# The inverse transform's residual rows: from two row groups of 512 columns to four row groups of 256, with the heads' banks taken in turn

## The chip, the cores and the metric

The program runs on one core of a Trainium2 chip. The metric is the time on the device, in microseconds, of one execution of the whole program. Several runs of each kernel are taken, and their median is compared. One execution is also recorded by the hardware profiler, and the profile lines come from that one. Engines are named as in the profile: PE (TensorE's matmuls), PEld (its weight loads), DVE (VectorE), ACT (ScalarE), POOL (GpSimd), SP (the engine that issues most transfers). Times within an execution are counted from the start of its span.

## What is computed

The input is 128 graphs of 128 nodes with 256 channels each, and an adjacency matrix per graph. Two layers follow one another; each is added to its input. All arithmetic is float32.

```python
# layer 0
h = max(layernorm(x), 0)
x = x + L0(h, adj)
#   L0: xc = h^T;  c1 = relu(bn1(conv1d(xc, conv1_w, width 1)))
#       c2 = bn2(conv1d(c1, conv2_w, width 17, pad 8))
#       x_conv = relu(c2 + xc)^T
#       s = h @ w_se^T + b_se;  A = exp(-|s_n - s_m|^2) * adj
#       x_nmp = A @ relu(h @ w_msg^T + b_msg)
#       a GRU cell with input [x_conv, x_nmp] and state h gives the output
# layer 1: five graph convolutions on subsets of the first 25 nodes, weighted and summed
h = max(layernorm(x), 0)
x = x + L1(h, adj)
```

## The kernel before

The 128 graphs are worked in 32 blocks of four (`BB = 4`, `N = 128` nodes, `T = 512` columns, `H = 256`).

**The heads** (up to about 277 us). Block by block, `head_stats`, `head_norm`, `head_turn` and `head_conv1` do the layer norm, the transpose and the width-1 convolution; `head_spectra` takes the result to the frequency domain by a matmul with `fd`. In between, `some_spectra` runs one round of `weight_spectra` at a time: the taps of the width-17 convolution go to the frequency domain (L164, 17 rows, four row groups of the array into four banks; the copies out of the banks are L170 on DVE and L172 on ACT) and to DRAM as `vd`. `constants()` prepares the two batch norms: it has two steps, and the second one scales the weights `wc1` (L136) that `head_conv1` (L227) multiplies by. All of this stands under a manual schedule, so each engine works in the order written.

**The products per frequency** (277 to 455 us). `spectral` loads `v` from `vd`, multiplies for each of 68 frequency pairs, and writes `yd` (the first 128 of 136 rows) and `yrd` (the last eight, the residual rows).

**The main part** (from 455 us). For each block the GRU's gates are computed by seven products per unit (L636). Between two products the generator `beside_gates` does a step of the next block: `messages` (L522, emptied by L532 to L541), then `conv_out` in two steps, `edge_terms` (L560), `edges` (L572: four matmuls of 5 rows on four row groups, into four banks), `x_nmp` (L587); or a step of `back` (L800, L813) or of `layer1` (L904, L964).

`conv_out` is the inverse transform of the width-17 convolution: for each half `o` of the channels it sums the residual rows `yr` (eight per graph, times `idr`, L499) and the 128 main rows `ym` (times `idm`, L502) in one bank of PSUM, then DVE scales the bank and adds `ht` (L504), and ACT applies the relu (L505). In the kernel before, the residual rows of the four graphs lie in 32 partitions for each `o`; one matmul of 512 columns with a block-diagonal `idr` serves the four graphs. `load_y` loads `ym` and `yr` two blocks ahead.

PSUM has eight banks; `bank()` gives one. All of them come from one pool with eight buffers under one name. In the compiled program of the kernel before, a bank is given out again in the order in which banks come free in the compiler's plan, and PE's instructions stand in the order of the program text.

Of the kernel before, what the change touches and what calls it, by code (L numbers as in the profile page):

```python
# [8 lines left out]
F32 = mybir.dt.float32  # L9
# [4 lines left out]
P = 128  # L14
# [3 lines left out]
BB = 4  # L18
# [56 lines left out]
def gnn_kernel(ctx: ExitStack, tc: tile.TileContext, io, out0: bass.AP, out1: bass.AP):  # L75
# [8 lines left out]
    front = ExitStack()  # L84
    hc = front.enter_context(tc.tile_pool(name="hc", bufs=1))
    dram = ctx.enter_context(tc.tile_pool(name="dram", bufs=1, space=bass.MemoryType.DRAM))
    psum = ctx.enter_context(tc.tile_pool(name="psum", bufs=8, space=bass.MemoryType.PSUM))

    def bank():
        return psum.tile([P, 512], F32, tag="bank", name="bank")  # L90

    def row(name, n):

# [21 lines left out]
    def constants():  # L115


        for j, v0 in enumerate((V_BN1, V_BN2)):
            g, b, m, v = (vec[:, v0 + 2 * q:v0 + 2 * q + 2] for q in range(4))
            sc, sh = bn[:, j, 0, :], bn[:, j, 1, :]  # L120
            ve = cst.tile([P, C], F32, name=f"bnve{j}")
            nc.vector.tensor_scalar(ve, v, EPS, None, op0=ALU.add)
            rs = cst.tile([P, C], F32, name=f"bnrs{j}")
            nc.gpsimd.tensor_tensor(rs, ve, mhalf[:, :C], op=ALU.pow)
            nc.vector.tensor_mul(sc, g, rs)
            nc.vector.tensor_mul(ve, m, sc)
            nc.vector.tensor_sub(sh, b, ve)

        bnb = hc.tile([P, 2 * C, P], F32, name="bnb")
        nc.vector.tensor_copy(bnb, bn[:, 0].rearrange("p q c -> p (q c)")[:, :, None].to_broadcast([P, 2 * C, P]))  # L130
        yield
        psb = bank()
        for q in range(2 * C):
            nc.tensor.matmul(psb[:, q * P:(q + 1) * P], bnb[:, q, :], ident, start=True, stop=True)
        nc.scalar.copy(bnr.rearrange("p q d -> p (q d)"), psb)
        nc.vector.tensor_mul(wc1, wc1, bnr[:, 0:1, :].to_broadcast([P, C, D]))  # L136
        nc.vector.tensor_add(brz, vec[:, V_IH:V_IH + 4], vec[:, V_HH:V_HH + 4])
        yield

# [9 lines left out]
    def taps_load(pool, c, q, queue, split=1, amid=None):  # L149
        w2 = pool.tile([P, WCH // 4, P], F32, tag="w2", name="w2", bufs=3)  # L150
        for t in range(0, WCH // 4, WCH // 4 // split):
            queue.dma_start(w2[:, t:t + WCH // 4 // split], io["w2t"][:, c, q, t:t + WCH // 4 // split])
            if amid:
                amid.pop()()
        return w2
# [198 lines left out]
    with front as es:  # L354
# [9 lines left out]
        with ExitStack() as ws:  # L364

            ws.enter_context(tc.manual_schedule())

            xk = ws.enter_context(tc.tile_pool(name="xk", bufs=1, side="right"))
            wp = ws.enter_context(tc.tile_pool(name="wp", bufs=1))
            ahead = 4  # L370
            todo = [(c, q) for c in range(C) for q in range(D // WCH)]
            nc.scalar.dma_start(gt, io["gt"])
            nc.scalar.dma_start(vec, io["vec"])

            taps = [taps_load(wp, *todo[0], nc.sync, split=4, amid=[lambda: head_load(xk, ahead, 0, nc.sync)])]
            spectra = []

            def some_spectra(k=1):
                for _ in range(k):
                    if not spectra and todo:  # L380
                        spectra.append(weight_spectra(wp, *todo.pop(0), taps.pop(0)))
                    if spectra and next(spectra[0], STOP) is STOP:
                        spectra.pop(0)
                        if len(todo) > 2:
                            taps.append(taps_load(wp, *todo[2], nc.sync))
                        some_spectra()

            constant_loads()
            head_load(xk, ahead, 1, nc.sync)
            taps.append(taps_load(wp, *todo[1], nc.sync))  # L390
            for k in range(2, ahead):
                head_load(xk, ahead, k, nc.sync)
            nc.sync.dma_start(fw, row("fw", 5))
            taps.append(taps_load(wp, *todo[2], nc.sync))
            head_stats(hk, 0)
            some_spectra()
            head_norm(0)
            consts = constants()
            next(consts)
            some_spectra()  # L400
            some_spectra()
            head_turn(hk, 0)
            head_stats(hk, 1)
            some_spectra()
            next(consts)
            head_norm(1)
            head_stats(hk, 2)
            some_spectra()
            heads(hk, xk, ahead, X, some_spectra)
            while spectra or todo:  # L410
                some_spectra()

        bp = es.enter_context(tc.tile_pool(name="bp", bufs=1, reuse_waits="tile"))
        spectral(bp, (X0, 0), 0, NB, {})
# [46 lines left out]
    def load_y(i):  # L461
        g0 = i * BB
        yr = wk.tile([P, P], F32, tag="yr", name="yr", bufs=2)
        ym = wk.tile([P, BB, D], F32, tag="ym", name="ym", bufs=2)
        nc.sync.dma_start(ym, yd[g0:g0 + BB].rearrange("g r o -> r g o"))
        for o in range(C):
            nc.sync.dma_start(yr[o * BB * NR:(o + 1) * BB * NR, :],
                              yrd[g0:g0 + BB, :, o * P:(o + 1) * P].rearrange("g r o -> (g r) o"))
        loaded[i] = ym, yr

    fmx = cst.tile([P, 1], F32)
# [19 lines left out]
    def conv_out(i):  # L491

        ht = hts[i]
        ym, yr = loaded.pop(i)
        xc = wk.tile([P, C, T], F32, tag="xc", name="xc", bufs=2)
        pss = [bank() for _ in range(C)]
        for o, ps in enumerate(pss):
            g = slice(o * BB * NR, (o + 1) * BB * NR)
            nc.tensor.matmul(ps, yr[g, :], idr[g, :], start=True, stop=False)  # L499
        for o, ps in enumerate(pss):  # L500
            for b in range(BB):
                nc.tensor.matmul(ps[:, b * N:(b + 1) * N], ym[:, b, o * P:(o + 1) * P], idm,  # L502
                                 start=False, stop=b == BB - 1)
            nc.vector.scalar_tensor_tensor(xc[:, o, :], ps, sc2[:, o:o + 1], ht[:, o, :], op0=ALU.mult, op1=ALU.add)  # L504
            nc.scalar.activation(xc[:, o, :], xc[:, o, :], AF.Relu, bias=sh2[:, o:o + 1])  # L505
            yield
        xcs[i] = xc
# [505 lines left out]
    with tc.manual_schedule(engines={nc.gpsimd.engine}):  # L1013
# [2 lines left out]
        nc.gpsimd.memset(lr, 0.0)  # L1016
        nc.gpsimd.memset(lr[:, 0, :, 3:4], -1.0)
        nc.gpsimd.memset(lr[:, 1, :, 4:5], 1.0)
    idr = wk.tile([P, T], F32)
    nc.sync.dma_start(idr[:C * BB * NR], io["idr"])  # L1020

    load_y(0)
    load_y(1)
# [75 lines left out]
def _spectral_constants():  # L1099
# [24 lines left out]
    inv[0, 0], inv[0, 1] = c[0] / LW, c[NP_] / LW  # L1124
    inv[1:, 0], inv[1:, 1] = 2 * c[f] / LW, -2 * s[f] / LW
    inv = inv.reshape(LW, P)
    idr = np.zeros((2, BB, NR, BB, P))
    for b in range(BB):
        idr[:, b, :, b] = inv[P:]
    d = {"gt": gt.reshape(P, LW), "fd": fd.reshape(P, LW), "idm": inv[:P], "idr": idr.reshape(2 * BB * NR, BB * P)}  # L1130
    return {k: np.ascontiguousarray(v, dtype=np.float32) for k, v in d.items()}


# [86 lines left out]
```

## Time and profile before

| | |
|---|---|
| median of 3 runs | 1884.16 us (1883.59 to 1886.41) |
| the profiled execution | 1882.45 us |
| its span, first to last instruction | 1880.5 us |
| PE busy | 1858.3 us, 99% of the span |
| DVE, ACT, POOL busy | 1353.7, 743.4, 665.3 us |
| mean granted clock of TensorE | 0.998 |

A group's line in the profile reads: line of the code, engine, operation, output<-inputs, shapes, count, then busy time in us and mean ns of one, then the engine's idle time just before these instructions and what ended most of it. A float32 matmul leaves two records. "Released by" is inferred from semaphores. In the timeline each row has its start, its length, the engine and the line; in brackets stands the idle time before it and what ended it.

### The profile page before, as it was taken

How to read it: one execution, taken by the hardware profiler on the slowest of the kernel's cores; microseconds unless marked ns; L12 is line 12 of the kernel's file. 1: busy time of each engine (PE TensorE's matmuls, PEld its weight loads, DVE VectorE, ACT ScalarE, POOL GpSimd, SP SyncE). 2: the span in 40 equal slices, each digit the busy share in tenths (PEclk: the TensorE clock that was granted, in tenths of full speed). 3: DMA queues.
4: the chain of work that ended last, by engine and by line, in shares of the span. 5: the costliest groups of instructions: out<-in, count | busy, mean ns of one | idle time of the engine just before them, and what ended most of it. 6: DMA issues, size and time to landing. Idle time of an engine off the chain costs nothing.

```text
span 1880.5 us, 31012 instructions
## 1 busy us (share of the span) xinstructions
PE 1858.3 (99%) x10854; PEld 1593.0 (85%) x10854; DVE 1353.7 (72%) x3248; ACT 743.4 (40%) x1667; POOL 665.3 (35%) x803
## 2 busy tenths in 40 slices
PE   8999999999999999999999999999999999999998
PEld 6888888888888888888788888888788888888887
DVE  7787765455878888888656778787666678788643
ACT  4665651111443334333334433433343343334334
POOL 1111125676343544454212345444312344544200
PEclk9999999999999999999999999999999999999999
DMA  8878788997532233224234322333233333222125
GB/s 295 292 309 309 283 291 280 349 314 248 165 90 73 72 83 94 76 72 121 64 103 113 122 74 72 90 79 112 61 102 94 121 94 86 72 72 67 41 88 157
DMA packets 218330, 267.95 MB, mean 142 GB/s; under 512 B 105186, under 2 KB 181815, under 8 KB 216127
## 3 DMA queue, kind: packets, MB, share of 16 engines
q1 hardware_dynamic: 206079, 195.60, 36.1%
q10 hardware_dynamic: 12096, 70.36, 9.1%
q8 instruction: 87, 1.43, 0.3%
q14 instruction: 68, 0.56, 0.1%
HBM read 169.24 MB, written 96.67 MB: 141 GB/s over the span
## 4 chain that ended last, share of the span: by engine, by line
PE 93%; DVE 2%; DMA 2%; POOL 1%; issue 0%; SPq 0%; ACT 0%; DVEq 0%; POOLq 0%; ACTq 0%
PE bank L636 44%; PE bank L318 6%; PE bank L227 5%; PE bank L964 5%; PE bank L904 5%; PE bank L522 5%; PE bank L502 3%; PE bank L243 3%; PE bank L313 3%; PE bank L587 3%; PE bank L164 2%; PE bank L499 2%; PE bank L213 1%; PE bank L883 1%; PE bank L813 1%; PE bank L572 1%
## 5 line engine op out<-in xcount | busy, mean ns | idle before, releaser
L636 PE MATMUL bank<-t,sw 128*128 128x256 f32 x1152 | 290.9, 379 | 0.0
L649 POOL TENSOR_TENSOR u<-u,m 128x256 f32<-128x256 f32 x128 | 93.4, 730 | 499.2 <-ACT m L647 424.6
L636 PEld LDWEIGHTS bank<-t,sw 128*128 128x128 f32 x1152 | 210.6, 190 | 26.6 <-issue 2.3
L636 PE MATMUL bank<-t,wih 128*128 128x256 f32 x768 | 197.2, 379 | 0.0
L636 PEld LDWEIGHTS bank<-t,wih 128*128 128x128 f32 x768 | 143.4, 190 | 19.3 <-issue 0.5
L227 PE MATMUL bank<-wc,ht 128*128 128x256 f32 x512 | 125.5, 390 | 0.3 <-DVE wc L136 0.3
L310 POOL TENSOR_TENSOR vs<-v 128x256 f32<-128x256 f32 x134 | 98.1, 756 | 72.4 <-PE bank L313 38.1
L545 ACT ACTIVATE msg<-msg 128x512 f32<-128x512 f32 x64 | 36.9, 622 | 205.5 <-DVE msg L541 205.5
L636 PE MATMUL bank<-xc,wih 128*128 128x256 f32 x384 | 114.5, 380 | 0.0
L636 PE MATMUL bank<-t,whh 128*128 128x256 f32 x384 | 114.5, 380 | 0.0
L636 PE MATMUL bank<-xn,wih 128*128 128x256 f32 x384 | 114.2, 379 | 0.0
L964 PE MATMUL bank<-w,hh 128*125 128x256 f32 (+9 forms) x480 | 113.3, 379 | 0.0
L197 POOL TENSOR_TENSOR rs<-ve,mhalf 128x4 f32<-128x4 f32 x32 | 32.6, 1020 | 223.0 <-DVE ve L195 223.0
L636 PE MATMUL bank<-ht,whh 128*128 128x256 f32 x384 | 109.9, 380 | 0.0
L904 PE MATMUL bank<-ax,w 128*128 128x500 f32 (+8 forms) x416 | 107.0, 396 | 0.9 <-DMA w<-in_w_dram 0.9
L227 PEld LDWEIGHTS bank<-wc,ht 128*128 128x128 f32 x512 | 93.6, 192 | 15.3 <-DVE wc L136 0.6
L964 PEld LDWEIGHTS bank<-w,hh 128*125 128x125 f32 (+9 forms) x480 | 84.3, 177 | 18.0 <-issue 0.9
L682 ACT ACTIVATE nn<-nn,vec 128x512 f32<-128x512 f32 x64 | 46.2, 722 | 134.1 <-DVE nn L681 134.1
L307 DVE SCALAR_TENSOR_TENSOR s<-X 128x256 f32<-128x256 f32 x67 | 46.2, 691 | 66.5 <-PE bank L318 66.5
L654 DVE TENSOR_TENSOR u<-bank,u 128x256 f32<-128x256 f32 x128 | 53.5, 418 | 54.5 <-PE bank L636 54.2
L172 ACT COPY sp<-bank 128x272 f32<-128x272 f32 x208 | 66.7, 401 | 63.0 <-PE bank L164 61.9
L502 PEld LDWEIGHTS bank<-idm,ym 128*128 128x128 f32 x512 | 66.0, 196 | 26.4 <-issue 24.0
(206 smaller groups left out, 4449.0 us busy)
## 6 DMA issues: line engine op xcount, KB each, us to landing
vd<-sp ACTq DMA_DIRECT2D x16, 2176.0 KB
v<-vd SPq DMA_DIRECT2D x34, 1024.0 KB
w<-in_w_dram SPq DMA_DIRECT2D x40, 512.0 KB
ln<-in_x_dram SPq DMA_DIRECT2D x32, 512.0 KB
htd<-ht ACTq DMA_DIRECT2D x32, 512.0 KB
yd<-ys ACTq DMA_DIRECT2D x32, 512.0 KB
ht<-htd SPq DMA_DIRECT2D x32, 512.0 KB
ym<-yd SPq DMA_DIRECT2D x32, 512.0 KB
```

Of the source, the lines that this page charges most:

```text
L172: nc.scalar.copy(dst, s)
L227: nc.tensor.matmul(pv[:, bb, :], ht[:, c, b * N:(b + 1) * N], wc1[:, c, :], start=c == 0, stop=c == C - 1)
L243: nc.tensor.matmul(ps[:, bb * LW:(bb + 1) * LW], h1[:, 2 * h + bb, c * P:(c + 1) * P], fd, start=True, stop=True)
L310: nc.gpsimd.tensor_tensor(vs[:, c], vr[c], vi[c], op=ALU.add)
L313: nc.tensor.matmul(p1[:, :D], a[:, c], vs[:, c], start=c == 0, stop=c == C - 1)
L318: nc.tensor.matmul(ps[:, k * D:(k + 1) * D], u[:, c], w[c], start=c == 0, stop=c == C - 1)
L502: nc.tensor.matmul(ps[:, b * N:(b + 1) * N], ym[:, b, o * P:(o + 1) * P], idm, start=False, stop=b == BB - 1)
L522: nc.tensor.matmul(ps[:, b, :], d[:, b * N:(b + 1) * N], w, start=True, stop=True)
L636: nc.tensor.matmul(ps, w, d, start=n == 0, stop=n == len(pairs) - 1)
L649: nc.gpsimd.tensor_tensor(got["u4"], got["u2"], got["m5"], op=ALU.add)
L904: nc.tensor.matmul(pv[:, q - q0, :], w1s[k5 + g][:, c, q * P:(q + 1) * P], xv[:, c], start=c == 0, stop=c == C - 1)
L964: nc.tensor.matmul(ps[:n1, :D], hh[:, q, at:at + n1], w2s[k5 + g][:, q, :], start=q == 0, stop=q == HID // P - 1)
```

## The change

It has three parts.

1. `conv_out`: the residual rows of each half `o` are split again by pairs of graphs, `h`. The four groups of 16 rows start at partitions 0, 32, 64 and 96. Each is one matmul of 256 columns into a bank of its own, of which half is used. The main rows' matmuls go to the same four half banks, and DVE empties each half bank by itself. `load_y` loads `yr` in four pieces; `idr` is laid out for this.
2. In the heads, `bank()` takes eight single-buffer banks in turn; after the heads that pool is closed and one with eight buffers under one name, and waits for each buffer, is opened.
3. `constants()` has three steps now: the first batch norm's scales are computed ahead of the first `head_stats`, the scaled weights ahead of the first `head_norm`, and the second batch norm's scales after the third `head_stats`. One round of `some_spectra` ahead of `heads` is left out (the rounds after it make up for it).

```diff
-    psum = ctx.enter_context(tc.tile_pool(name="psum", bufs=8, space=bass.MemoryType.PSUM))
+    turns = ExitStack()
+    banks = [turns.enter_context(tc.tile_pool(name="turns", bufs=1, space=bass.MemoryType.PSUM)), 0]
     def bank():
-        return psum.tile([P, 512], F32, tag="bank", name="bank")
+        pool, n = banks
+        if n is None:
+            return pool.tile([P, 512], F32, tag="bank", name="bank")
+        banks[1] = (n + 1) % 8
+        return pool.tile([P, 512], F32, tag=f"bank{n}", name="bank")
...
     def constants():
-        for j, v0 in enumerate((V_BN1, V_BN2)):
+        def scales(j, v0):
...
+        scales(0, V_BN1)
         bnb = hc.tile([P, 2 * C, P], F32, name="bnb")
...
         nc.vector.tensor_mul(wc1, wc1, bnr[:, 0:1, :].to_broadcast([P, C, D]))
+        yield
+        scales(1, V_BN2)
         nc.vector.tensor_add(brz, vec[:, V_IH:V_IH + 4], vec[:, V_HH:V_HH + 4])
         yield
...
+            consts = constants()
+            next(consts)
             head_stats(hk, 0)
             some_spectra()
+            next(consts)
             head_norm(0)
-            consts = constants()
-            next(consts)
             some_spectra()
             some_spectra()
             head_turn(hk, 0)
             head_stats(hk, 1)
             some_spectra()
-            next(consts)
             head_norm(1)
             head_stats(hk, 2)
-            some_spectra()
+            next(consts)
             heads(hk, xk, ahead, X, some_spectra)
             while spectra or todo:
                 some_spectra()
+        turns.close()
+        banks[:] = [ctx.enter_context(tc.tile_pool(name="psum", bufs=8, space=bass.MemoryType.PSUM, reuse_waits="tile")), None]
...
         for o in range(C):
-            nc.sync.dma_start(yr[o * BB * NR:(o + 1) * BB * NR, :],
-                              yrd[g0:g0 + BB, :, o * P:(o + 1) * P].rearrange("g r o -> (g r) o"))
+            for h in range(2):
+                r0, g1 = 32 * (2 * o + h), g0 + 2 * h
+                nc.sync.dma_start(yr[r0:r0 + 2 * NR, :],
+                                  yrd[g1:g1 + 2, :, o * P:(o + 1) * P].rearrange("g r o -> (g r) o"))
...
-        pss = [bank() for _ in range(C)]
-        for o, ps in enumerate(pss):
-            g = slice(o * BB * NR, (o + 1) * BB * NR)
-            nc.tensor.matmul(ps, yr[g, :], idr[g, :], start=True, stop=False)
-        for o, ps in enumerate(pss):
-            for b in range(BB):
-                nc.tensor.matmul(ps[:, b * N:(b + 1) * N], ym[:, b, o * P:(o + 1) * P], idm,
-                                 start=False, stop=b == BB - 1)
-            nc.vector.scalar_tensor_tensor(xc[:, o, :], ps, sc2[:, o:o + 1], ht[:, o, :], op0=ALU.mult, op1=ALU.add)
+        pss = [[bank()[:, :H] for _ in range(2)] for _ in range(C)]
+        for o in range(C):
+            for h, ps in enumerate(pss[o]):
+                r0 = 32 * (2 * o + h)
+                g = slice(r0, r0 + 2 * NR)
+                nc.tensor.matmul(ps, yr[g, :], idr[g, :], start=True, stop=False)
+        for o in range(C):
+            for h, ps in enumerate(pss[o]):
+                for b in range(2):
+                    nc.tensor.matmul(ps[:, b * N:(b + 1) * N], ym[:, 2 * h + b, o * P:(o + 1) * P], idm,
+                                     start=False, stop=b == 1)
+                v = slice(h * H, (h + 1) * H)
+                nc.vector.scalar_tensor_tensor(xc[:, o, v], ps, sc2[:, o:o + 1], ht[:, o, v], op0=ALU.mult, op1=ALU.add)
             nc.scalar.activation(xc[:, o, :], xc[:, o, :], AF.Relu, bias=sh2[:, o:o + 1])
             yield
...
-    idr = wk.tile([P, T], F32)
-    nc.sync.dma_start(idr[:C * BB * NR], io["idr"])
+    idr = wk.tile([P, H], F32)
+    nc.sync.dma_start(idr, io["idr"])
...
-    idr = np.zeros((2, BB, NR, BB, P))
-    for b in range(BB):
-        idr[:, b, :, b] = inv[P:]
+    idr = np.zeros((4, 32, 2, P))
+    for b in range(2):
+        idr[:, b * NR:(b + 1) * NR, b] = inv[P:]
```

More of the change, by code (lines that the diff above doesn't have):

```diff
@@ L1126, in _spectral_constants @@
     inv = inv.reshape(LW, P)
[L1127 to L1130 removed]
+    idr = np.zeros((4, 32, 2, P))
+    for b in range(2):
+        idr[:, b * NR:(b + 1) * NR, b] = inv[P:]
+    d = {"gt": gt.reshape(P, LW), "fd": fd.reshape(P, LW), "idm": inv[:P], "idr": idr.reshape(P, 2 * P)}
     return {k: np.ascontiguousarray(v, dtype=np.float32) for k, v in d.items()}
```

## The prediction

> **What bounds the kernel now.** I read the page first: the busy shares and the chain that ended last.
>
> ```profile
> span 1880.5 us, 31012 instructions
> ...
> PE 1858.3 (99%) x10854; PEld 1593.0 (85%) x10854; DVE 1353.7 (72%) x3248; ACT 743.4 (40%) x1667; POOL 665.3 (35%) x803
> ...
> PE 93%; DVE 2%; DMA 2%; POOL 1%; issue 0%; SPq 0%; ACT 0%; DVEq 0%; POOLq 0%; ACTq 0%
> ```
>
> TensorE is the bound nearly everywhere, so a change pays by what it takes off PE's own sequence, and costs by what makes PE wait. Next come the groups kept apart by shape, for the line that is changed (L499) and for a line that already uses four row groups in four banks (L572).
>
> ```profile
> L499 PE MATMUL bank<-idr,yr 32*128 32x512 f32 x128 | 36.7, 646 | 1.7 <-DMA yr<-yrd 1.7
> ...
> L572 PE MATMUL bank<-lt 5*128 5x128 f32 x256 | 16.4, 326 | 0.0
> ```
>
> Each float32 matmul leaves two records: L499's 64 matmuls are x128. "Busy, mean" is blurred by overlap, so the price is taken from the chain, in order of time, in one block of the steady part (blocks follow at 36.94 us):
>
> ```profile
> 774.09 1.06 PE bank L499 x4
> 775.15 1.09 PE bank L502 x8
> ...
> 781.89 0.43 PE bank L572 x8
> ```
>
> The pair of L499 holds PE 1.06 us per block; four L572 matmuls of 128 columns hold it 0.43. The timeline of the same block shows who has the banks:
>
> ```profile
> 774.02 1.13 PE L499 MATMUL bank<-idr,yr 32*128 32x512 f32 x4
> ...
> 773.59 0.41 DVE L644 TENSOR_TENSOR u<-bank,m 128x256 f32<-128x256 f32 x1
> 773.92 0.41 DVE L539 TENSOR_TENSOR msg<-bank,u 128x260 f32<-128x260 f32 x1
> 774.26 0.41 DVE L540 TENSOR_TENSOR u<-bank,u 128x260 f32<-128x260 f32 x1
> 774.77 0.43 DVE L541 TENSOR_TENSOR msg<-u,bank 128x260 f32<-128x260 f32 x1
> ```
>
> The reader is to see that at 774.02, where PE reaches L499, DVE is behind: it still empties banks that PE filled up to 3.6 us before. Last, PE's waits in the heads (23 to 300 us), and one of them in the timeline:
>
> ```profile
> PE bank L164 <- DVE h L230: 3.0, 7, 0.4
> PE bank L164 <- DVE X L251: 0.5, 2, 0.3
> ...
> 36.55 0.50 PE L164 MATMUL bank<-gt,w 17*128 17x136 f32 x4
> 37.47 0.73 PE L164 MATMUL bank<-gt,w 17*128 17x136 f32 x12 [0.42 <-DVE h L230]
> ```
>
> Of four row groups two ran both halves (x4) and the third waited for its bank. So a row group whose bank is late does not hold those issued ahead of it, but all behind it.
>
> **What the Trainium skill says.** "TensorEngine Tiling (Array Packing)", Key Properties: different tiles run their weight loads and matmuls in parallel, and a change of tiling mode drains the array. The trace agrees: L572's eight records would take 8 x 0.111 = 0.89 us one after another (L502, full rows, 128 columns, takes 0.89 for eight) and take 0.43. The same page, Gotcha 1: row tiles that run together write different banks. That is why the new form needs four banks at once. "TensorE: Matmul & The Clock Gate", Part 3, gives 3.07 times for four row groups of 512 columns; no run here has that shape. Its Part 1 says that the clock falls to half after an idle window; here it was 0.50 from 462 to 468 us, after the 1.74 us wait for yr ahead of the first L499.
>
> **Part 1: the residual rows.** A 256-column record streams for 0.216 us (L636: 12 in 2.59). Before: weights 0.11, two halves of 512 columns at 0.427, 0.09 to the next line in full mode (L502 starts at 775.08), 1.06 in all. After, with all four banks free: 0.11 + 2 x 0.216 + 0.02 for the stagger of four starts + 0.09 = 0.65. Saving 0.41 us per block, on the path, since nothing else can use PE meanwhile.
>
> But which banks? The eight go round in the order in which they come free. Counting back through the matmuls ahead of L499, the oldest free ones are those emptied by L534, L641, L644 and L539; today the pair takes the first two, long free. The third comes free at 774.00, the fourth when L539 ends, 774.33. A bank's release reaches PE 0.06 later (L230 ends at 37.41, L164 starts at 37.47). So three groups run at once, the fourth starts at 774.39, needs 0.11 + 0.43 + 0.09 = 0.63 alone, and L502 starts at 775.02 in place of 775.08: **0.06 is left of 0.41**. By the timeline L539 stands at this place in 25 of the 32 blocks: 1.5 us. In five (480.95, 943, 1010, 1382, 1449) it ended over 2 us ahead: 5 x 0.41 = 2.05. In two (885.7, 1324.8) it ends 0.70 after: 0.76 + 0.63 - 1.06 = 0.33 lost, 0.65. In the first block the rows come by four loads at 0.41 us of SP instead of two, right behind the write of yrd, and PE waits for them: about 0.5 lost at half clock. Sum: **-2.4 us**. Bounds for the fourth bank: no wait at all (-0.41), or one or two evictions later (L540, L541; see the rivals). I take L539, because PE issues in program order throughout and DVE's order ahead of this place is untouched.
>
> DVE: two evictions of 0.74 (512 columns) become four. A TENSOR_TENSOR from a bank takes 0.41 for 256 and 0.69 for 512 columns, so half of 0.74 is about 0.47, and issued back to back a pair ends 0.1 to 0.2 later. DVE idles 17% of 470 to 1840 us, which hides 10 us of it. What is late next: L504, L505, L647, L649, L651 hang in a row, and the bank that L651 frees at 784.11 is wanted at 784.38. Those 0.27 cover it; without them it costs 0.1 per block. The number of L502 matmuls and ACT's relu stay. SP issues 64 more loads of 0.41 us, 26 us of a queue that is far ahead (two blocks); idr keeps its bytes. The banks of the second half stay taken until its second step; in that stretch the smallest margins are 0.5 us or more.
>
> **Part 2: banks in the heads.** Now each of eight single buffers is used in turn, so a bank comes back eight allocations later. The seven waits above are for banks given back only three allocations before; the bank of eight before had been free 3.8 us. They go: 3.0, and the two on L251 0.5. One place would wait newly (L227 at 176.4, where ACT's copies are 2 us late): 0.6. Sum -2.9. What is next is PE itself: over 22 to 277 us DVE is busy 196 of 255. The new pool after the heads starts behind its banks' last users, which empty up to 0.7 us after PE's last head matmul: I take +0.3.
>
> **Part 3: constants.** L122 to L130 stood between the first norm and the second stats on DVE (10.60 to 13.90, 3.3 us, with two round trips to POOL). One trip now stands ahead of the first stats. The vec transfer ends at about 5.4 (SP's wait for it), ln at 5.6, so stats start 1.8 later; L136 adds 0.7, partly beside POOL's power; the second trip, behind the third stats (and behind its power on POOL), holds the first L230 about 1.5 to 2 us. Against it the PE waits before L227 (0.6) and at 22.57 (0.74, a bank) go, and one round of L164 moves behind. Net -1.3, bounds +1 and -2.5: the chain up to 22.57 us is DVE's.
>
> **Sum.** -2.4 - 2.9 + 0.3 - 1.3 = -6.3 us. The profiled execution took 1882.45 (span 1880.5 and 1.95 around it): 1876.15. The median of the runs is 1.71 above it, so **1877.9**. What a measurement of this kernel can tell from no change is about 0.2%, 3.8 us.
>
> **Rivals.**
> *No bank wait* (0.14): DVE has emptied L539's bank in time. Then 32 x 0.41 less the 0.5, and 3.9 from the front: -16.5, 1867.7. For it: DVE is only 0.37 late; against it: the same lateness in 25 blocks.
> *The front gives nothing* (0.16): transfers load the DMA engines at 81 to 85% up to 455 us and a late v holds PE at 361 (1.0 us); what the heads gain waits there. Left is -2.4: 1881.8.
> *Slower by the fourth bank* (0.14): it is one that frees later. With L540 (ends 774.67) L502 starts at +1.34, 0.28 lost in 25 blocks, 7.0, against 4.8 gained elsewhere (3.9 at the front, 2.05, less 0.65 and 0.5): +2.2, 1886.4. With L541 (775.20) 0.81 x 25 = 20: +15, 1899. It decides from an eviction that ends 0.56 us after PE's arrival. For it: the two are next in the row; against it: four banks, and L539 is the fourth.
> *Four groups do not overlap* (0.02): 8 x 0.216 = 1.73 against 1.06, +21; L572 and L164 speak against it.
>
> **Numbers.** My case has 0.54, its own range 1874 to 1881.5. The range, 1867.5 to 1886.5, takes in the first two rivals and the constants' bounds. Faster by over 0.2%: most of my case and the first rival, 0.66. Within 0.2%: most of the second, 0.17. Slower: 0.17.
>
> **What would show it.** L499 as x8 of 256 columns per block, three groups together and the fourth some 0.37 us later, waiting for DVE L539; L502 at 1.00 us after L499's start; no PE wait on L230 in the heads; L302 about 4 us earlier than 277.0. Wrong if all four start within 0.03 us (no wait), if the fourth waits for L540 or L541, or if L302 is not earlier.

## The result, and the profile after

The changed kernel took 1887.80 us (median of 13 runs, 1883.88 to 1894.79), the kernel before 1887.26 us (median of 13 runs, 1883.59 to 1889.03). The ratio is 1.001, its 95% interval 0.9999 to 1.002: no difference that can be told, where 6.3 us less was forecast. The ratio is worked out from all runs together and is not the quotient of the two medians; here and below, a difference in us is the ratio's, so it can lie a us or so off the difference of the medians beside it. The profiled execution of the changed kernel is one of its long ones (1892.84 us). It lies 10.4 us above the profiled execution of the kernel before, so the two spans must not be set against each other as they stand; the times of the runs and the periods within a trace decide.

Lines move with the change: L499 is L513, L502 L517, L504/L505 L520/L521, L539 L555, L572 L588, L636 L652, L647/L649/L651 L663/L665/L667, L813 L829, L164 L172, L230 L238, L227 L235, L302 L310.

The page of the changed kernel:

```profile
span 1891.0 us, 31451 instructions
...
PE 1863.2 (99%) x10982; PEld 1601.9 (85%) x10982; DVE 1359.9 (72%) x3312; ACT 745.7 (39%) x1667; POOL 666.6 (35%) x803
...
PE 92%; DMA 3%; DVE 2%; POOL 1%; issue 0%; ACT 0%; SPq 0%; ACTq 0%; DVEq 0%; POOLq 0%
```

PE is still the bound. DVE has 64 instructions more, the split evictions, and 6 us. The group of the residual rows (count, busy us, mean ns, then idle before and its releaser):

```profile
L513 PE MATMUL bank<-idr,yr 16*128 16x256 f32 x256 | 34.4, 434 | 3.0 <-DMA yr<-yrd 3.0
```

L513 leaves 256 records of 256 columns where L499 left 128 of 512. The wait for yr in the first block is 3.0 us (1.7 before). What the steady blocks do stands in the chain, in order of time:

```profile
778.92 0.99 PE bank L513 x8
779.92 1.09 PE bank L517 x8
...
788.15 0.72 PE bank L829 x4
788.87 3.25 PE bank L652 x14
```

and, of the kernel before, the piece that answers to the last line:

```profile
784.11 3.02 PE bank L636 x14
```

The first line is the forecast's: 0.99 for the residual rows, 1.06 before. The last is not: these 14 gate records took 3.02 us before and take 3.25 now. A steady block lasts 37.09 us against 36.94: 0.07 less at L513, 0.22 more behind L829. The timeline around L513 shows who has the fourth bank:

```profile
778.42 0.41 DVE L660 TENSOR_TENSOR u<-bank,m 128x256 f32<-128x256 f32 x1
778.76 0.41 DVE L555 TENSOR_TENSOR msg<-bank,u 128x260 f32<-128x260 f32 x1
...
778.86 1.06 PE L513 MATMUL bank<-idr,yr 16*128 16x256 f32 x8
779.09 0.42 DVE L556 TENSOR_TENSOR u<-bank,u 128x260 f32<-128x260 f32 x1
```

L555 ends at 779.17, and the fourth group starts 0.37 us after the first, at 779.23. The bank, its eviction and the release of 0.06 us are as forecast.

PE's waits of the whole execution, by what ended them (total us, times, longest); these three are the one at the first inverse, one in the heads and the one at the first product:

```profile
PE bank L513 <- DMA yr<-yrd: 3.0, 1, 3.0
PE bank L172 <- DVE h L238: 2.9, 1, 2.9
...
PE bank L310 <- DVE X L259: 0.8, 1, 0.8
```

The seven waits of 0.4 us on the add of h (L238) are gone, as forecast; one of 2.9 us has come in their place. The first spectral product (L310) starts at 277.04 us, where L302 started; about 4 us earlier was forecast. A single execution is a rough measure of the heads, though: the four other kernels below with these heads (heads_only, relu_half, later_half, later) start it between 273.6 and 276.5 us, the four with the heads of before (before, conv_only, split_stt, split_pin) between 276.6 and 278.5.

### The profile page after: what moved, and what is told of

The parts are those of the page before. It is cut to its first block, busy times and chain, and to the rows that moved or that the text cites. A ratio compares the mean times of both kernels' runs of the same rounds, so it can differ in the third digit from the quotient of the medians.

```text
span 1891.0 us, 31451 instructions
## 1 busy us (share of the span) xinstructions
PE 1863.2 (99%) x10982; PEld 1601.9 (85%) x10982; DVE 1359.9 (72%) x3312; ACT 745.7 (39%) x1667; POOL 666.6 (35%) x803
## 4 chain that ended last, share of the span: by engine, by line
PE 92%; DMA 3%; DVE 2%; POOL 1%; issue 0%; ACT 0%; SPq 0%; ACTq 0%; DVEq 0%; POOLq 0%
PE bank L652 45%; PE bank L235 6%; PE bank L326 5%; PE bank L980 5%; PE bank L920 5%; PE bank L538 5%; PE bank L517 3%; PE bank L251 3%; PE bank L603 3%; PE bank L321 3%; PE bank L172 2%; PE bank L513 2%; PE bank L221 1%; PE bank L899 1%; PE bank L829 1%; DMA v<-vd 1%
## 5 line engine op out<-in xcount | busy, mean ns | idle before, releaser
L652 PE MATMUL bank<-t,sw 128*128 128x256 f32 x1152 | 291.1, 380 | 0.0
L665 POOL TENSOR_TENSOR u<-u,m 128x256 f32<-128x256 f32 x128 | 94.1, 735 | 499.7 <-ACT m L663 421.4
L652 PEld LDWEIGHTS bank<-t,sw 128*128 128x128 f32 x1152 | 210.6, 190 | 26.7 <-issue 2.3
L652 PE MATMUL bank<-t,wih 128*128 128x256 f32 x768 | 197.2, 379 | 0.0
L652 PEld LDWEIGHTS bank<-t,wih 128*128 128x128 f32 x768 | 143.4, 190 | 19.3 <-DVE u L670 0.5
L235 PE MATMUL bank<-wc,ht 128*128 128x256 f32 x512 | 128.9, 397 | 0.9 <-ACT sp L180 0.9
L561 ACT ACTIVATE msg<-msg 128x512 f32<-128x512 f32 x64 | 37.0, 623 | 207.4 <-DVE msg L557 207.3
L652 PE MATMUL bank<-xc,wih 128*128 128x256 f32 x384 | 117.1, 386 | 0.0
L652 PE MATMUL bank<-t,whh 128*128 128x256 f32 x384 | 114.5, 380 | 0.0
L652 PE MATMUL bank<-xn,wih 128*128 128x256 f32 x384 | 114.2, 379 | 0.0
L235 PEld LDWEIGHTS bank<-wc,ht 128*128 128x128 f32 x512 | 95.6, 196 | 17.1 <-ACT sp L180 1.1
L652 PE MATMUL bank<-ht,whh 128*128 128x256 f32 x384 | 109.9, 380 | 0.0
L920 PEld LDWEIGHTS bank<-ax,w 128*128 128x128 f32 x416 | 69.9, 190 | 19.4 <-issue 12.1
```

What stands on the lines that cost most here:

```text
L235: nc.tensor.matmul(pv[:, bb, :], ht[:, c, b * N:(b + 1) * N], wc1[:, c, :], start=c == 0, stop=c == C - 1)
L652: nc.tensor.matmul(ps, w, d, start=n == 0, stop=n == len(pairs) - 1)
L665: nc.gpsimd.tensor_tensor(got["u4"], got["u2"], got["m5"], op=ALU.add)
L920: nc.tensor.matmul(pv[:, q - q0, :], w1s[k5 + g][:, c, q * P:(q + 1) * P], xv[:, c], start=c == 0, stop=c == C - 1)
```

## The experiments

**The parts one by one.** Part 1 alone is the kernel before with the new conv_out, load_y and idr.

> The kernel before with part 1 alone (conv_out, load_y, idr); the heads' banks and the constants stay as before. Theory A (the late eviction): each steady block is longer, because DVE empties the two half banks of the second step later, ACT's relu of the whole 512 columns starts later, and ACT's next copy, POOL's add and DVE's add behind it give a gate's bank back some 0.2 us after PE wants it. Then the start of the residual rows to the main rows takes 0.98 us (1.06 before), the piece of gate products that follows the matmul on ae is 3.25 us (3.02), a steady block lasts 37.09 us (36.94), and from the first inverse to the end it is 4 to 6 us longer than before. In all 1.001 to 1.004 of before. Rival B (the new pool of banks after the heads brings the wait): here that pool is as before, so the piece stays at 3.02, a block lasts 36.88, and the kernel is 1 to 3 us faster. Both: the first spectral product stays at 277.0 us.

Measured: 1889.65 us against 1885.61; ratio 1.0023, interval 1.0016 to 1.0031, so +4.3 us. The residual rows take 0.98, the way from the matmul on ae to x_nmp 3.96 (3.74 before), a steady block 37.09: theory A has it. The new pool is not in this kernel: rival B falls. From the first inverse to the end it is 3.9 us longer, but that number alone would prove little, since the four kernels with the old conv_out (before, turns_only, consts_only, heads_only) lie between 1418.6 and 1427.3 us there; the period of the steady blocks is what repeats. Its first spectral product started at 278.5, and its first inverse at 467.0 in place of 461.1, although up to 455 us it issues the same work in the same order as the kernel before. Of the 5.9 us only 1.3 belong to the change (PE waits 3.0 us for yr in place of 1.7). The rest is one execution against another: the front is 1.4 us longer, and PE waits 2.95 us for v at 354 us, with a clock of 0.59 over the next 4 us, where the kernel before waits 0.3 and 1.0 at full clock.

Part 2 alone:

> The kernel before with part 2 alone: the heads' banks in turn, a new pool after the heads. Theory A: the seven PE waits of 0.4 us on the add of h are gone, with no wait of 2 to 3 us at 26 us, as the constants stand as before; the first spectral product starts 2 to 3.5 us earlier than 277.0. The transfers of v, which run at some 390 GB/s there, then hold PE longer at 345 to 365 us, so that the first inverse starts at most 1.5 us earlier than 461.1; the whole 0 to 2 us faster. Rival E (the gain of the heads arrives at the end): the first inverse 2.5 us earlier and the whole 2.5 us faster.

Measured: 1880.84 against 1886.51; 0.9978, interval 0.9969 to 0.9987, so -4.2 us. The first spectral product starts at 271.15, 5.9 us earlier, more than either theory said; the first inverse 3.2 us earlier. PE's waits between 23 us and the first spectral product fell from 3.5 to 0.9 us. Rival E has it: most of this reaches the end.

Part 3 alone:

> The kernel before with part 3 alone: the constants in three steps; banks as before. Theory A: here too the second batch norm's scales stand ahead of the first add of h, PE waits 2 to 3 us at about 26 us and runs at half clock behind it; the seven waits of 0.4 us stay; the first spectral product starts at 278 to 280 us (277.0 before), the whole is 1 to 3 us slower. Rival C (the constants gain 1.3 us, as the prediction had it): the first spectral product at 275.7.

Measured: 1888.62 against 1886.51; 1.0017, interval 1.0008 to 1.0026, so +3.2 us. The first spectral product starts at 283.35, 6.3 us late and later than theory A's 278 to 280; rival C falls. The waits on the add of h are there again, with the long one among them:

```profile
PE bank L167 <- DVE h L233: 5.4, 7, 2.2
```

Parts 2 and 3 together:

> The kernel before with parts 2 and 3 (the heads' banks in turn and the constants in three steps); conv_out as before. Theory A: the second batch norm's scales stand on DVE ahead of the first add of h; PE waits 2.9 us for it at about 26 us and then runs at half clock for some 10 us, which uses up what the seven waits of 0.4 us give. The first spectral product starts at 277 (+-0.5) us, steady blocks last 36.94 us, and the whole is within 2 us of before, unless the loads of v between 345 and 365 us cost more. Rival C (the prediction's sum; the wait in the changed kernel's profile came from that one execution): the first spectral product starts at 273 us and the whole is 3 to 5 us faster.

Measured: 1886.05 against 1885.61; 1.0006, interval 0.9993 to 1.0018. The first spectral product starts at 276.5, the steady block lasts 36.94; theory A has it. Part 3 takes back what part 2 gives. The three parts alone sum to +4.3 - 4.2 + 3.2 = +3.3 us; the whole change measured +1.9, with an interval of -0.2 to +3.8.

**The 0.22 us behind L829.** The relu for each half bank:

```diff
                 nc.vector.scalar_tensor_tensor(xc[:, o, v], ps, ...)
-            nc.scalar.activation(xc[:, o, :], xc[:, o, :], AF.Relu, bias=sh2[:, o:o + 1])
+                nc.scalar.activation(xc[:, o, v], xc[:, o, v], AF.Relu, bias=sh2[:, o:o + 1])
```

> The changed kernel with one edit: ACT's relu of conv_out is issued for each half bank, behind that half's eviction, so the first relu starts while DVE empties the second half. Theory A: ACT is free for its next copy some 0.2 us earlier; the piece of gate products behind the matmul on ae falls from 3.25 to 3.0 to 3.1 us, a steady block from 37.09 to about 36.9 us, and from the first inverse to the end it is 4 to 5 us shorter than the changed kernel. Rival D (the wait is a matter of banks, not of ACT's queue): 3.25 and 37.09 stay.

Measured: 1880.71 against 1885.61; 0.9976, interval 0.9968 to 0.9984. A steady block lasts 36.89, 0.05 under the kernel before, which is what the forecast's 0.06 asked for: theory A has it. Three timelines of the same place, from the second step's main rows to the gate products behind the wait, the rows of the chain alone. First the kernel before (the lines under their old numbers):

```profile
779.97 1.05 PE L502 MATMUL bank<-idm,ym 128*128 128x128 f32 x8
780.08 0.47 DVE L808 TENSOR_SCALAR hn<-bank,mv 100x256 f32<-100x256 f32 x1
781.09 0.74 DVE L504 SCALAR_TENSOR_TENSOR xc<-bank,bn,ht 128x512 f32<-128x512 f32 x1
781.87 0.72 ACT L505 ACTIVATE xc<-xc,bn 128x512 f32<-128x512 f32 x1 [0.53 <-DVE xc L504]
782.50 0.35 ACT L647 COPY m<-bank 128x256 f32<-128x256 f32 x1
783.69 0.42 DVE L651 TENSOR_TENSOR nh<-bank,u 128x256 f32<-128x256 f32 x1 [1.52 <-POOL u L649]
784.38 0.59 PE L636 MATMUL bank<-xc,wih 128*128 128x256 f32 x2
```

then the changed kernel:

```profile
784.74 1.05 PE L517 MATMUL bank<-idm,ym 128*128 128x128 f32 x8
785.05 0.47 DVE L824 TENSOR_SCALAR hn<-bank,mv 100x256 f32<-100x256 f32 x1
786.07 0.87 DVE L520 SCALAR_TENSOR_TENSOR xc<-bank,bn,ht 128x256 f32<-128x256 f32 x2
786.97 0.72 ACT L521 ACTIVATE xc<-xc,bn 128x512 f32<-128x512 f32 x1 [0.66 <-DVE xc L520]
787.60 0.35 ACT L663 COPY m<-bank 128x256 f32<-128x256 f32 x1
788.79 0.42 DVE L667 TENSOR_TENSOR nh<-bank,u 128x256 f32<-128x256 f32 x1 [1.52 <-POOL u L665]
789.26 0.30 PEld L652 LDWEIGHTS bank<-xc,wih 128*128 128x128 f32 x2 [0.36 <-DVE nh L667]
```

then relu_half:

```profile
779.54 0.87 DVE L520 SCALAR_TENSOR_TENSOR xc<-bank,bn,ht 128x256 f32<-128x256 f32 x2
780.05 0.91 ACT L521 ACTIVATE xc<-xc,bn 128x256 f32<-128x256 f32 x2 [0.27 <-DVE xc L520]
780.86 0.35 ACT L663 COPY m<-bank 128x256 f32<-128x256 f32 x1
782.05 0.42 DVE L667 TENSOR_TENSOR nh<-bank,u 128x256 f32<-128x256 f32 x1 [1.32 <-POOL u L665]
782.53 0.30 PEld L652 LDWEIGHTS bank<-xc,wih 128*128 128x128 f32 x2 [0.15 <-DVE nh L667]
```

Follow the last line's releaser upwards: the weight load waits for DVE's L667, that for POOL's add L665, that for ACT's copy L663, and L663 has nothing to do with conv_out except that it stands behind its relu on ACT. From L520's start to L663's it is 1.53 us in the changed kernel and 1.32 in relu_half.

Is it the late eviction, or that four banks are taken? The kernel before, with its two full banks, each emptied in two instructions:

```diff
-            nc.vector.scalar_tensor_tensor(xc[:, o, :], ps, ...)
+            for h in range(2):
+                w = slice(h * (T // 2), (h + 1) * (T // 2))
+                nc.vector.scalar_tensor_tensor(xc[:, o, w], ps[:, w], ...)
```

> The kernel before with one edit: DVE empties each full bank of conv_out by two instructions of 256 columns in place of one of 512. PE's matmuls, the banks and the loads stay. Theory A (the late eviction is what costs): the residual rows still hold PE for 1.06 us, the piece of gate products behind the matmul on ae grows from 3.02 to 3.2 us, a steady block from 36.94 to 37.1 us, and the whole is 3 to 5 us slower. Rival D (the wait comes from four banks being taken in place of two): 3.02 and 36.94 stay, and the time is that of before.

Measured: 1884.76 against 1885.61; 0.9994, interval 0.9986 to 1.0003, a steady block 36.94. Taken alone these numbers are those of rival D; the timeline says why they don't refute theory A:

```profile
780.23 0.87 DVE L506 SCALAR_TENSOR_TENSOR xc<-bank,bn,ht 128x256 f32<-128x256 f32 x2
780.98 0.37 ACT L647 COPY m<-bank 128x256 f32<-128x256 f32 x1 [0.51 <-PE bank L636]
781.25 0.73 ACT L507 ACTIVATE xc<-xc,bn 128x512 f32<-128x512 f32 x1
```

The copy (L647) now runs ahead of the relu (L507): with another eviction before it, the compiler ordered ACT's work anew, and the chain was cut. So the experiment had changed two things. With the copy pinned at its old place:

```diff
-                    nc.scalar.copy(got["m5"], ps)
+                    tc.keep_in_program_order(nc.scalar.copy(got["m5"], ps))
```

> split_stt with one more edit: the copy of the gates' fifth product (m5) is pinned behind the instruction that stands ahead of it on ACT in the text. In split_stt the compiler had put this copy ahead of the second relu of conv_out; now ACT's order is that of the kernel before, and the only difference from it is that DVE empties each full bank of conv_out in two instructions. Theory A (the chain from the last eviction over the relu, the copy m5, POOL's add and DVE's add to the bank is what costs): the last eviction ends some 0.27 us later than before, the bank comes 0.05 us after PE wants it, the weight load behind the wait is no longer hidden, and the way from the matmul on ae to x_nmp takes 3.85 to 3.96 us in place of 3.74; a steady block 37.05 to 37.15 us in place of 36.94, the whole 3 to 5 us slower than before. Rival D (it takes four banks): 3.74 and 36.94.

Measured: 1889.38 against 1884.70; 1.0024, interval 1.0018 to 1.0031. The way from ae to x_nmp takes 3.89, a steady block lasts 37.09. The chain, in order of time:

```profile
786.52 3.19 PE bank L636 x14
```

Two banks, full-width residual rows, the old order, and the loss is there: it is the split eviction ahead of the relu and the copy, and not the number of banks. (The pin alone was not run; but ACT's order is that of the kernel before, and the whole 0.15 by which the block is longer lies on the way from ae to x_nmp.)

The two ways differ, 3.89 us here and 3.96 in conv_only, and yet a block lasts 37.09 in both. From the start of the residual rows to the end of the last eviction it is 7.8 us in the kernel before and 8.06 to 8.08 in split_pin, conv_only and the changed kernel: DVE is done no sooner for PE's shorter residual rows. So the 0.07 that PE saves at L513 it waits for again at this bank, and in these blocks the fourth bank gains nothing.

**The fourth bank.** conv_out one product later (the kernel `later`), which should find DVE caught up:

```diff
             next(ends, None)
             yield
+            yield
             inverse = conv_out(i) if i else iter(())
...
             edges(i)
             yield
             next(ends, None)
             yield
-            yield
             yield from x_nmp(i)
```

First on top of relu_half:

> The changed kernel with the relu for each half bank, and one edit more: a step without work between messages and conv_out, and one idle step less behind edges, so that conv_out's two steps, edge_terms and edges run one product later. Theory A (the fourth half bank waits for DVE's backlog from the tail of the block before): one product later DVE has caught up, all four groups start within 0.03 us, the residual rows hold PE for 0.64 us in the steady blocks in place of 0.98, and a block lasts 36.5 to 36.6 us in place of 36.89. Rival F (DVE's work only moves: what is won at the residual rows is waited for at the next bank, since the evictions of conv_out come later by a product): 0.64 there, but a block lasts 36.8 us or more.

Measured: 1874.51 against 1886.51; 0.9943, interval 0.9931 to 0.9955. All four groups start within 0.03 us, 0.64 in every block after the first, a steady block 36.60: theory A has it, rival F falls. Then without the split relu:

> The changed kernel with one edit: conv_out's steps, edge_terms and edges one product later; the relu stays whole (512 columns), the constants stay as in the changed kernel. Theory A (the relu costs because it stands ahead of the copy m5 on ACT): one product later the copy m5 is ahead of the second relu, so the whole relu holds nobody up; the residual rows take 0.64 us, no new wait stands behind the matmul on ae, and a steady block lasts 36.6 us as in later_half; about 0.994 to 0.995 of before. Rival J (a whole relu comes too late for edges' exps or the gates' inputs in any place): a steady block lasts 36.7 us or more.

Measured: 1872.52 against 1884.35; 0.9936, interval 0.9922 to 0.9949. A steady block lasts 36.53 us, a little less than with the split relu, and rival J falls. That is 0.41 us under the kernel before, which is what the prediction gave for four free banks. The timeline of `later`, one block, shows both effects:

```profile
807.76 0.41 DVE L555 TENSOR_TENSOR msg<-bank,u 128x260 f32<-128x260 f32 x1
...
808.61 0.42 DVE L557 TENSOR_TENSOR msg<-u,bank 128x260 f32<-128x260 f32 x1
...
810.08 0.71 PE L513 MATMUL bank<-idr,yr 16*128 16x256 f32 x8
...
814.66 0.38 ACT L663 COPY m<-bank 128x256 f32<-128x256 f32 x1
...
816.49 0.72 ACT L521 ACTIVATE xc<-xc,bn 128x512 f32<-128x512 f32 x1
```

L557, the last of these evictions from a bank, is over 1.0 us before L513, so no group waits; and the copy L663 is now 1.8 us ahead of the second relu, so a whole relu delays nobody.

**The second scales.** The part of `constants` that needs POOL's power goes between later rounds of the heads:

```diff
+            if wait:
+                yield
             nc.vector.tensor_mul(sc, g, rs)
...
-            next(consts)
-            heads(hk, xk, ahead, X, some_spectra)
+            def between():
+                some_spectra()
+                rounds[0] += 1
+                if rounds[0] in (9, 11):
+                    next(consts)
+            heads(hk, xk, ahead, X, between)
```

> The changed kernel with the relu for each half bank, and one edit more: the second batch norm's scales are taken out of the start of the heads and put between later rounds (the part ahead of POOL's power at the ninth round, the rest at the eleventh). Theory A: the PE wait of 2 to 3 us at 26 us falls to under 1 us, no half clock follows, and the first spectral product starts 2 to 3 us earlier than in relu_half (274.4), at about 272. If the transfers of v then take what is won, the first inverse stays within 1 us of 460.4; if not, it starts at about 458 and the whole is 2 us faster than relu_half.

Measured: 1877.77 against 1886.51; 0.9957, interval 0.9945 to 0.9969. The first spectral product starts at 270.55 (274.38 in relu_half), the first inverse at 456.6 (460.4): theory A has it, and what is won arrives. What happened in the changed kernel, in its timeline:

```profile
22.70 0.16 DVE L127 TENSOR_SCALAR bnve<-vec 128x2 f32<-128x2 f32 x1
22.87 1.01 POOL L205 TENSOR_TENSOR rs<-ve,mhalf 128x4 f32<-128x4 f32 x1 [3.83 <-DVE bnve L127]
23.85 0.70 POOL L129 TENSOR_TENSOR bnrs<-bnve,mhalf 128x2 f32<-128x2 f32 x1
24.58 0.16 DVE L130 TENSOR_TENSOR bn<-vec,bnrs 128x2 f32<-128x2 f32 x1 [1.72 <-POOL bnrs L129]
25.12 0.68 DVE L238 TENSOR_TENSOR h<-bank,bnr 128x512 f32<-128x512 f32 x1
...
25.86 1.29 PE L172 MATMUL bank<-gt,w 17*128 17x136 f32 x16 [2.92 <-DVE h L238]
```

DVE stands still for 1.72 us, because POOL must first do the third block's power; the first add of h waits behind that, and PE 2.9 us behind the add. Then the clock: PE's busy time, the granted clock, DMA share and GB/s, in stretches of 6 us, first of the changed kernel, then of mid_half:

```profile
24.00:30.00 6.00, 4.14 (x23) 0.64 0.70 281
30.00:36.00 6.00, 6.00 (x30) 0.51 0.00 0
```

```profile
24.00:30.00 6.00, 5.66 (x48) 1.00 0.69 273
30.00:36.00 6.00, 6.00 (x61) 1.00 0.83 252
```

The changed kernel does 30 records from 30 to 36 us, all of them busy time, where mid_half does 61. PE reads as fully busy in both: only the clock and the count tell the loss. For relu_half the two costs can be estimated from its trace: PE waits 1.9 us there, and the clock of 0.78 and 0.93 over the same two stretches takes 6 x 0.22 + 6 x 0.07 = 1.7 us, together 3.6 of the 3.8 us that mid_half gains.

**The versions put together.** All three edits, then the same with part of the first block's loads on ACT:

```diff
-                nc.sync.dma_start(yr[r0:r0 + 2 * NR, :],
+                (nc.sync if i or h else nc.scalar).dma_start(yr[r0:r0 + 2 * NR, :],
```

> The changed kernel with three edits together: the relu for each half bank, conv_out one product later, the second batch norm's scales between later rounds of the heads. Theory A (the terms add up): first spectral product at 270.6 us, first inverse at 456.6, steady blocks of 36.6 us, a span of about 1869 us, 0.992 of before. Rival G (what is won at the front is waited for later): the first inverse at 459 or later, 0.994 of before.

> The kernel best with one edit more: of the first block's four loads of yr, the first of each pair of graphs is issued by ACT, so SP has two in place of four behind the write of yrd. Theory H (the first inverse waits 3.0 us, where the kernel before waits 1.7, because four loads follow one another on one queue): the wait falls to about 1.7 us, the half clock behind it stays or gets shorter, and the whole is 1.3 to 3 us faster than best. Rival I (the wait is the transfer's own time after the write of yrd): 3.0 stays, and the time is that of best.

Measured for the first: 1872.21 against 1884.70; 0.9934, interval 0.992 to 0.9947. Its trace is what the sum asked for (270.6, 457.0, 36.60, span 1869.7); the ratio lies between the two theories. For the second: 0.9931, interval 0.9917 to 0.9946, and PE still waits 3.2 us, now for something else (in this kernel's lines: L489 loads yr, L561 and L665 copy banks out, L523 is the residual rows):

```profile
456.32 0.81 ACTq L489 DMA_DIRECT2D yr<-yrd  x2
457.17 0.38 ACT L561 COPY m<-bank 128x260 f32<-128x260 f32 x1 [8.29 <-DMA yrd<-ys]
...
458.20 1.01 PE L523 MATMUL bank<-idr,yr 16*128 16x256 f32 x2 [3.20 <-ACT m L665]
```

ACT's loads have to wait for the write of yrd, and ACT's copies stand behind them; PE waits for these copies. So the run doesn't tell theory H from rival I, and why the wait is longer stays open. What is shown: the wait was 1.3 to 1.8 us in all six kernels with two loads and 2.9 to 3.4 us in all nine with four on SP.

Last, `later` with the scales moved, and with the constants of the kernel before:

> The kernel later (conv_out one product later, the relu whole) with the second batch norm's scales between later rounds of the heads. Theory A (the terms add up): first spectral product at 270.6 us in place of 274.8, steady blocks of 36.53 us, a span of 1866 us, about 0.991 of before. Rival G (the transfers of v take what the front wins): the first inverse stays at 460, 0.9935.

> As later_mid, but with the constants in two steps as in the kernel before (parts 1 and 2 of the change and the later conv_out, without part 3). Theory K (the rest of part 3 gains nothing: the early scales delay the first statistics by what they save later): first spectral product at 270.6 to 271.5 us as in turns_only, the time within 1 us of later_mid. Rival C (the rest of part 3 gains the 1.3 us forecast): first spectral product at 272 us or later and 1 to 2 us slower than later_mid.

Measured: 1870.66 and 1871.75 against 1886.31; 0.9919 (0.9903 to 0.9935) and 0.9921 (0.9908 to 0.9935). later_mid has the shortest span of all, 1867.4, and is faster than both the kernel before and the changed one, but is not told apart from later_oc (theory K): the rest of part 3 gains nothing that these runs can tell. The first inverse of later_mid starts at 456.5, so its rival G falls. The first spectral product started at 269.75 and 271.63; the other kernels with the scales moved had 270.55, 270.61 and 272.08, and turns_only, with the constants as before, 271.15.

## Why the prediction was wrong, by its own steps

The forecast was -6.3 us, the change measured +1.9 (-0.2 to +3.8). Three terms failed, all of them costs put too low: the relu chain behind the evictions, the constants and the first block's loads. The mechanism of the fourth bank was right.

| step of the sum | forecast | what the runs showed |
|---|---|---|
| steady blocks, fourth bank | -0.06 in 25 blocks, waits for L539 | -0.07 in 23, waits for L555, the same eviction |
| five blocks with free banks | -0.41 each | 0.64 in place of 1.06: -0.42 |
| two late blocks | +0.33 each | 1.37 to 1.38: +0.31, in three blocks |
| first block | +0.5 | PE's wait for yr 3.0 in place of 1.7: **+1.3** |
| relu chain behind the evictions | 0, at most 0.1 per block | **+0.22 in 24 blocks** |
| banks in turn, new pool | -2.6 | -4.2 (-5.8 to -2.5) |
| constants | -1.3, bounds +1 and -2.5 | **+3.2 (1.5 to 4.9)** |

The first five rows come to 23 x -0.07 - 5 x 0.42 + 3 x 0.31 + 1.3 + 24 x 0.22 = +3.8 us, where part 1 alone measured +4.3 (3.0 to 5.8) and -2.4 was forecast.

**The relu chain.** The prediction named the chain and its cover, 0.27 us, and then let the cover hold, because a pair of evictions ends only "0.1 to 0.2 later". Counted from the second step's first main-row matmul, the last eviction ended at 1.86 us before and at 2.19 after: 0.33 later. The pair itself gives 0.13 of it (0.87 for two halves against 0.74). The other 0.20 is there ahead of it: DVE's scaling of hn (L808 before, L824 after) starts at 0.11 before and 0.31 after. 0.13 to 0.14 of that is the first step's pair, as split_pin shows (hn at 0.25, the last eviction at 2.12 to 2.13), and the last 0.06 to 0.07 is no lateness of DVE's but PE's own shorter residual rows. Of the 0.33 the cover took 0.27; the bank's release took 0.05 to reach PE (789.21 to 789.26), so the matmul started 0.11 late. The next gap on PE grew by another 0.10: a weight load that had been beside the matmul ahead of it now follows the wait. Together 0.22 per block; 24 of the 30 ways from ae to x_nmp grew by it, some 5.3 us. The prediction had sized the delay for one pair and the price for one wait, and each block has two pairs and two gaps; and it booked PE's gain at the residual rows and DVE's delay as separate terms, where the one adds to the wait on the other. Its figure for DVE's idle time, 17% of 470 to 1840 us, does not come out of the trace either (1029.75 us busy of 1370, so 25%); but idle time on the whole says nothing about a stretch in which DVE is behind. relu_half and split_pin show the chain from both sides; that the second gap is the weight load is read from the trace and was not tested by itself.

**The constants.** The prediction saw that the first add of h would be held "about 1.5 to 2 us" and set against it other waits that would go. It did not ask what PE does meanwhile. PE stood for 2.9 us, and the clock was 0.64 and then 0.51 up to 36 us. One of the waits set against it was also smaller than put: the one ahead of L227 was 0.3 us on PE's own row, and 0.6 on that of the weight load. The prediction had itself cited the Trainium skill, "TensorE: Matmul & The Clock Gate", Part 1, and the half clock at 462 us after a wait of 1.74 us, and used it for the first block alone. By the lower bound of what the part cost alone (1.5 us), even the prediction's own bound of +1 was too low.

**The first block.** The prediction let PE wait 0.5 us longer for four loads in place of two. The wait grew by 1.3 us in the changed kernel. Why two loads more, at 0.41 us of SP each, cost so much stays open, as best_yr did not tell. Nor is PE's order in this block that of the text, as the prediction took it to be throughout: one main-row matmul (466.54) stands between the first group (465.68) and the other three (467.26).

**The heads' banks.** Forecast -2.6; the first spectral product came 5.9 us earlier and the whole 4.2. The waits that a row of the profile names were 3.5 us; shorter gaps went too, since from each start to the next the records of L164 take 58.9 us up to the first spectral product in the kernel before and 51.0 in turns_only. The new pool's term was too small on the other side: in every kernel with it PE waits 0.8 us at the first spectral product, for DVE's last eviction of X, where the kernels with the old pool show no gap; +0.3 was taken.

**The rivals.** In number, "slower by the fourth bank" came nearest, with its 1886.4 for L540. That nearness is luck: it looked for the loss at the residual rows, in the bank that L540 empties, but there the fourth group waits for L555 (the old L539) as in the forecast; the loss is at a bank of the gates some 10 us further on (789.26 against 778.86), through ACT and POOL. "The front gives nothing" (1881.8) was right that the front's gain would not be seen, but for another reason. It let the transfers of v take what the front gains, which holds in part at most: in turns_only 2.7 of 5.9 us are gone by the first inverse (PE waits 3.1 us at 346 us there), but mid_half's front is 3.8 us shorter than relu_half's and its first inverse starts 3.8 us earlier. What emptied the front was part 3. The rival's other half, a gain of 2.4 us in part 1, did not come.

## What to carry to other kernels

When an eviction is split or moved, follow what stands behind it in each engine's own order, to the next bank that the tensor engine wants, and price the lateness of the whole chain against its cover; an unrelated copy behind the same relu is enough to give back the gain. If that chain is what binds, time saved on the tensor engine ahead of it is waited for again. Where a wait is added on a busy tensor engine, ask for a stretch at half clock behind it too: here waits of 1.9 to 2.9 us at 26 us brought one in all six kernels that had them, and waits for v at the products in five kernels of eleven (PE's busy time does not show it, the count of records does). And when an experiment says no, look first whether it changed only what it meant to: here the compiler had turned two instructions round, and the pinned version gave the opposite answer.

## What the runs showed of the hardware that was not expected

- The length of a wait alone does not decide on the half clock behind it. In the heads, a wait of 2.9 us at 26 us gave 0.64 and 0.51 over the two stretches of 6 us (the changed kernel), one of 1.9 us at the same place 0.78 and 0.93 (relu_half). At the products, five kernels with a wait of 2.4 to 3.3 us for v had a clock of 0.57 to 0.59 over the next 4 us, with 11 records of PE (the changed kernel, conv_only, turns_only, consts_only, split_pin); six with one of 2.3 to 3.2 us kept 1.00, with 19 records (relu_half, later_half, mid_half, best, best_yr, later_mid). At the first inverse, waits of 1.3 to 3.4 us were followed by 0.50 within 4 us in all kernels but heads_only. What decides stays open.
- A bank that came 0.11 us late cost PE 0.22 (the changed kernel), one that came 0.06 late 0.15 (split_pin): the wait and a gap of about 0.10 after it.
- Splitting small work costs little on the engine itself: two evictions of 256 columns took 0.87 us against 0.74 for one of 512, two relus 0.91 against 0.72. What cost was who stood behind.
